# When the output projection follows the normalization, and which engine copies the convolution's image into PSUM

## The chip, the cores and the metric

The kernel runs on one core of one Trainium2 chip. The metric is the device time of one execution in microseconds; less is better. A profile of one execution is read beside it: busy times, waits and instructions of TensorE (PE), VectorE (DVE), ScalarE (ACT), GpSimd (POOL) and of the queue of SyncE (SP), which issues the transfers (DMA).

## The reference

Two layers on x of shape (4, 512, 64, 64), all in float32. Cut to what matters:

```python
# layer 0: attention over the 4096 pixels of an image, 128 channels inside
q, k, v = conv1x1(x, wq) + bq, conv1x1(x, wk) + bk, conv1x1(x, wv) + bv
attn = softmax(q^T k)                        # 4096 x 4096 for each of the 4 images
x = conv1x1(v attn^T, wo) + bo + x
# layer 1: involution, a 7x7 convolution whose weights are computed at each pixel
o = relu(conv1x1(x, W1) * s1 + b1)           # 128 channels in 8 groups of 16
w = conv1x1(relu(conv1x1(o, Wr) * sr + br), Ws) + bs     # 8 x 49 weights per pixel
o[c] = sum over 49 taps of w[group(c), tap] * shifted(o[c], tap)
x = conv1x1(o, W3) * s3 + b3 + x
```

## The kernel before

Each image (a batch) begins with its keys and values. Then its queries are worked through in 8 chunks of 512 pixels (8 image rows). For one chunk, 32 steps each make a score tile `pss`, its exponential `pt` on ScalarE, and add `v` times `pt` to `po` on TensorE; VectorE adds the exponentials into `pacc`. When the 32 steps are over, `finish_chunk` normalizes, projects and computes the tap weights; `involution` multiplies and adds the 49 taps; `close_chunk` projects and stores. These three are generators. They are not run at once: after each step of a later chunk, `chores` lets each of them make one turn, so that their instructions lie among those of the attention.

```python
    def takes(engine, us):
        free[engine] = max(free[engine], pe) + us
        return free[engine]
# ...
    def pace():
        nonlocal due, seen
        due, seen = min(due + TAPS_A_US * (pe - seen), 10), pe
        for _ in range(2):
            if due < 1 or not step(taps, 1):
                break
            due -= 1
# ...
    def chores():
        step(finishing, 1)
        step(closing, 1)
        pace()
```

`step` makes a turn of a generator; a turn that yields "wait" ends it without using up what is due. `pe` is the TensorE time issued so far by the kernel's own book, and `free` the time until which each of the others is booked. They decide only in which order instructions are issued.

The taps read the image `po1` from PSUM (8 rows and a border of 3 on each side). It is copied there from `o1` in SBUF: 11 rows at first, the last 3 when the next chunk's rows are known (`ready`). The weights of 7 taps come in one transfer `wb` of 1792 KB, read from the DRAM scratch `wsp`, into one of three buffers; two are loaded ahead.

```python
    def involution(b, c, o1):
        top = RW + PAD

        po1 = ps1.tile([P, RW + 2 * PAD, W + 2 * PAD], F32, tag="o1", name=f"po1_{b}_{c}")
        for _ in range(2):
            yield "wait"
        nc.scalar.copy(po1[:, :top], o1[:, :top])
        yield "wait"
        # ...
        for tap in range(NTAP):
            dy, dx = divmod(tap, K)
            if dx == 0:
                if dy == PAD + 1:
                    while (b, c) not in ready:
                        yield "wait"
                    yield "wait"
                    nc.scalar.copy(po1[:, top:], o1[:, top:])
                    yield "wait"
                wb, landed = loaded.pop(0)
                pump()
            while "tail" not in ready and (
                pe < landed or free["dve"] > pe + 3.0 or free["pool"] > pe + 6.0
            ):
                yield "wait"
            free["pool"] = max(free["pool"], takes("dve", DVE_OP))
            takes("pool", POOL_OP)
            prod = acc
            if tap:
                prod = prods.tile([P, RW, W], F32, tag="prod", name=f"prod_{b}_{c}_{tap}")
            nc.vector.tensor_tensor(
                prod, po1[:, dy : dy + RW, dx : dx + W],
                wb[:, dx, :].rearrange("p (r w) -> p r w", r=RW), ALU.mult,
            )
            if tap and "tail" in ready and tap % 2 and tap < NTAP - 2:

                first = accp is None
                if first:
                    accp = ps1.tile([P, CH], F32, tag="po", name=f"accp_{b}_{c}")
                mm(
                    accp, ident, prod.rearrange("p r w -> p (r w)"),
                    start=first, stop=tap == NTAP - 4,
                )
            elif tap:
                nc.gpsimd.tensor_tensor(acc, acc, prod, ALU.add)
            yield
```

The normalization takes the reciprocals of the sums, stores one row of them for a later check, and multiplies. The projection `pwo` follows after two turns:

```python
    def finish_chunk(b, c, o1s, po, sums):
        xt = xb[b, c]
        on = work2.tile([P, CH], F32, tag="on", name=f"on_{b}_{c}")
        nc.scalar.copy(on, po)
        for _ in range(3):
            yield
        pl = ps.tile([P, CH], F32, tag="mm", name=f"pl_{b}_{c}")
        mm(pl, ones, sums)
        rl = work1.tile([P, CH], F32, tag="rl", name=f"rl_{b}_{c}")
        for i in range(4):
            yield
            cols = slice(i * P, (i + 1) * P)
            takes("dve", 0.9)
            nc.vector.reciprocal(rl[:, cols], pl[:, cols])
        nc.sync.dma_start(rls[b * NCH + c : b * NCH + c + 1, :], rl[:1, :])
        takes("dve", DVE_OP)
        nc.vector.tensor_tensor(on, on, rl, ALU.mult)
        for _ in range(2):
            yield
        for t in range(CT):
            pw = ps.tile([P, CH], F32, tag="mm", name=f"pwo_{b}_{c}_{t}")
            mm(pw, w_slice(O_WO, t), on)
            takes("dve", DVE_OP)
            nc.vector.scalar_tensor_tensor(
                xt[:, t, :], pw, bo[:, t : t + 1], xt[:, t, :], ALU.add, ALU.add
            )
            yield
            if t % 2:
                yield
        p1 = ps.tile([P, RW, W], F32, tag="mm", name=f"p1_{b}_{c}")
        for t in range(CT):
            mm(
                p1.rearrange("p r w -> p (r w)"), w_slice(O_W1, t), xt[:, t, :],
                t == 0, t == CT - 1,
            )
            if t == 1:
                yield
        # ... relu, the image o1, the tap weights wc, their transfer to wsp,
        # and taps.append(involution(b, c, o1)) at its end
```

Once the last attention is over ("tail"), the taps go on with every other addition on TensorE instead of GpSimd.

Of the kernel before, what the change touches and what calls it, by code (L numbers as in the profile page):

```python
# [59 lines left out]
def fast_path(  # L60
# [18 lines left out]
    nc = tc.nc  # L79
# [41 lines left out]
# [3 lines that stand above are left out]
# [15 lines left out]
    def w_slice(off, t):  # L139
        return wt[:, off + t * P : off + (t + 1) * P]  # L140

    def v1(i):
        return vec[:, i : i + 1]

    def mm(o, lhsT, rhs, start=True, stop=True, shared=1):
        pe_us(rhs.free_size() * PE_COLUMN / shared)
        nc.tensor.matmul(o, lhsT=lhsT, rhs=rhs, start=start, stop=stop)  # L147
# [19 lines left out]
    def pump():  # L167
        while pending and len(loaded) < 2:
            wsp, written, i, name = pending.pop(0)
            wb = wbpool.tile([P, PIECE, CH], F32, tag="wb", name=name)  # L170
            nc.sync.dma_start(
                wb,
                wsp.rearrange("(g k) n -> g k n", g=G)[:, i * PIECE : (i + 1) * PIECE, :]
                .unsqueeze(0).broadcast_to([GC, G, PIECE, CH]),
            )
            free["dma"] = max(free["dma"], written)
            loaded.append((wb, takes("dma", PIECE_US) + LAND_US))
# [7 lines left out]
    def involution(b, c, o1):  # L185
        top = RW + PAD

        po1 = ps1.tile([P, RW + 2 * PAD, W + 2 * PAD], F32, tag="o1", name=f"po1_{b}_{c}")
        for _ in range(2):
            yield "wait"  # L190
        nc.scalar.copy(po1[:, :top], o1[:, :top])
        yield "wait"
        acc = work2.tile([P, RW, W], F32, tag="acc", name=f"acc_{b}_{c}")
        accp = None
        for tap in range(NTAP):
            dy, dx = divmod(tap, K)
            if dx == 0:
                if dy == PAD + 1:
                    while (b, c) not in ready:
                        yield "wait"  # L200
                    yield "wait"
                    nc.scalar.copy(po1[:, top:], o1[:, top:])
                    yield "wait"
                wb, landed = loaded.pop(0)
                pump()
            while "tail" not in ready and (
# [24 lines that stand above are left out]
        if accp is not None:  # L231
            nc.vector.tensor_tensor(
                acc, accp.rearrange("p (r w) -> p r w", r=RW), acc, ALU.add
            )
        closing.append(close_chunk(b, c, acc))
# [67 lines left out]
    def new_o1(b, c):  # L303
        o1 = o1pool.tile([P, RW + 2 * PAD, W + 2 * PAD], F32, tag="o1", name=f"o1_{b}_{c}")
        nc.gpsimd.memset(o1[:, :, :PAD], 0.0)
        nc.gpsimd.memset(o1[:, :, PAD + W :], 0.0)
        if c == 0:
            nc.gpsimd.memset(o1[:, :PAD, PAD : PAD + W], 0.0)
        if c == NCH - 1:
            nc.gpsimd.memset(o1[:, PAD + RW :, PAD : PAD + W], 0.0)  # L310
        return o1
# [16 lines that stand above are left out]
        nc.sync.dma_start(rls[b * NCH + c : b * NCH + c + 1, :], rl[:1, :])  # L328
        takes("dve", DVE_OP)
        nc.vector.tensor_tensor(on, on, rl, ALU.mult)  # L330
        for _ in range(2):
            yield
        for t in range(CT):
            pw = ps.tile([P, CH], F32, tag="mm", name=f"pwo_{b}_{c}_{t}")
# [3 lines that stand above are left out]
                xt[:, t, :], pw, bo[:, t : t + 1], xt[:, t, :], ALU.add, ALU.add  # L338
            )
            yield  # L340
            if t % 2:
                yield
        p1 = ps.tile([P, RW, W], F32, tag="mm", name=f"p1_{b}_{c}")
        for t in range(CT):
# [6 lines that stand above are left out]
        o1 = o1s[c]  # L351
        inner = o1[:, PAD : PAD + RW, PAD : PAD + W]
        nc.scalar.activation(inner, p1, AF.Relu, bias=v1(V_B1), scale=v1(V_S1))  # L353
        if c + 1 < NCH:
            o1s[c + 1] = new_o1(b, c + 1)
            nc.gpsimd.tensor_copy(  # L356
                o1s[c + 1][:, :PAD, PAD : PAD + W], o1[:, RW : RW + PAD, PAD : PAD + W]
            )
        if c > 0:
            nc.gpsimd.tensor_copy(  # L360
                o1s.pop(c - 1)[:, PAD + RW :, PAD : PAD + W], o1[:, PAD : 2 * PAD, PAD : PAD + W]
            )
        for t in range(CT):

            nc.scalar.activation(xt[:, t, :], xt[:, t, :], AF.Identity, bias=v1(V_B3 + t))  # L365
            if t % 2:
                yield
        pr = ps.tile([P, CH], F32, tag="mm", name=f"pr_{b}_{c}")
        mm(pr, wt[:, O_WR : O_WR + P], inner)
        red = work1.tile([P, CH], F32, tag="red", name=f"red_{b}_{c}")  # L370
        nc.scalar.activation(red, pr, AF.Relu, bias=v1(V_BR), scale=v1(V_SR))
        for _ in range(2):
            yield
        wc = work1.tile([P, 4, CH], F32, tag="wc", name=f"wc_{b}_{c}")
        for m0 in range(0, 4, 2):
            pcs = []
            for m in range(m0, m0 + 2):

                pc = ps.tile([P, CH], F32, tag="mm", name=f"pc_{b}_{c}_{m}")
                mm(  # L380
                    pc[:NWC, :], wt[CR * m : CR * (m + 1), O_WC : O_WC + NWC],
                    red[CR * m : CR * (m + 1), :], shared=2,
                )
                pcs.append(pc)
            for m, pc in zip(range(m0, m0 + 2), pcs):
                nc.scalar.activation(  # L386
                    wc[:NWC, m, :], pc[:NWC, :], AF.Identity,
                    bias=vec[:NWC, V_BC + m : V_BC + m + 1],
                )
            yield  # L390
        wsp = scratch.tile([4 * NWC, CH], F32, tag="wsp", name=f"wsp_{b}_{c}")
        written = takes("dma", WC_US) + LAND_US
        nc.sync.dma_start(wsp.rearrange("(m r) n -> r m n", m=4), wc[:NWC])
        pending.extend((wsp, written, i, f"wb_{b}_{c}_{i}") for i in range(NTAP // PIECE))
        pump()
        if c > 0:
            ready.add((b, c - 1))
        if c == NCH - 1:
            ready.add((b, c))
        taps.append(involution(b, c, o1))  # L400


# [458 lines left out]
```

## Time and profile before

| | |
|---|---|
| time, median of 3 | 2904.59 us (2897.92 to 2905.29) |
| span of the profiled execution | 2896.9 us |
| mean granted TensorE clock | 0.972 |
| one score or value product (2 passes) | 1.02 us, one each 0.86 us |
| ScalarE copy to `po1`, 11 rows (128x770) | 32 of 805 ns, 25.8 us |
| ScalarE copy to `po1`, 3 rows (128x210) | 32 of 338 ns, 10.8 us |
| one tap on VectorE, `prod` (128x512) | 1536 of 681 ns, 1001.0 us |
| one addition of a tap on GpSimd, `acc` | 1488 of 1270 ns, 1889.9 us |
| reciprocals `rl` on VectorE (128x128) | 128 of 929 ns, 115.6 us |

A line of a wait list says which engine and line waited for which other engine and line, then the us in total, the number of times and the longest. A line of a timeline has the start in us, the duration, engine, line, operation, tiles out<-in, shapes and how many it merges; in brackets stand the idle time just before it and who ended it. L330 is the multiplication `on`, L202 and L191 are the two copies to `po1`, L147 is every matmul. "PEld" is the load of TensorE's weights.

### The profile page before, as it was taken

How to read it: one execution, taken by the hardware profiler on the slowest of the kernel's cores; microseconds unless marked ns; L12 is line 12 of the kernel's file. 1: busy time of each engine (PE TensorE's matmuls, PEld its weight loads, DVE VectorE, ACT ScalarE, POOL GpSimd, SP SyncE). 2: the span in 40 equal slices, each digit the busy share in tenths (PEclk: the TensorE clock that was granted, in tenths of full speed). 3: DMA queues.
4: the chain of work that ended last, by engine and by line, in shares of the span. 5: the costliest groups of instructions: out<-in, count | busy, mean ns of one | idle time of the engine just before them, and what ended most of it. 6: DMA issues, size and time to landing. Idle time of an engine off the chain costs nothing.

```text
span 2896.9 us, 23193 instructions
## 1 busy us (share of the span) xinstructions
PE 2702.9 (93%) x6250; PEld 1150.1 (40%) x6250; DVE 1919.7 (66%) x3016; ACT 954.5 (33%) x1569; POOL 1916.3 (66%) x1623
## 2 busy tenths in 40 slices
PE   8999999999899999999989999999989999999975
PEld 4444443343344444443434444443334444444421
DVE  0447777876456777777464777777636577777864
ACT  2333333332233333333223333333233333333310
POOL 0028877777734877887780777778865288777744
PEclk9999999999999999999999999999999999999987
DMA  6048888889937988888991989998895588888896
GB/s 213 15 100 180 205 202 194 202 200 226 237 84 183 198 199 202 199 202 203 253 215 41 213 199 207 204 202 206 213 242 139 123 201 201 201 189 189 188 229 167
DMA packets 97532, 540.84 MB, mean 187 GB/s; under 512 B 6640, under 2 KB 6768, under 8 KB 68592
## 3 DMA queue, kind: packets, MB, share of 16 engines
q1 hardware_dynamic: 97104, 538.01, 79.5%
q8 instruction: 51, 0.84, 0.1%
q10 hardware_dynamic: 288, 1.27, 0.1%
q14 instruction: 89, 0.73, 0.1%
HBM read 479.94 MB, written 59.24 MB: 186 GB/s over the span
## 4 chain that ended last, share of the span: by engine, by line
PE 37%; DMA 33%; POOL 14%; DVE 10%; issue 5%; ACT 1%; SPq 0%; POOLq 0%; DVEq 0%; ACTq 0%
DMA wb<-wsp 31%; POOL acc L229 13%; PE pss L147 11%; PE po L147 11%; PE py L147 4%; DVE pacc L439 4%; PE p L147 4%; DVE prod L215 3%; PE pwo L147 3%; DVE rl L327 2%; DMA wsp<-wc 2%; PE pv L147 1%; PE pk L147 1%; PE pq L147 1%; DMA out_dram<-xb 0%
## 5 line engine op out<-in xcount | busy, mean ns | idle before, releaser
L229 POOL TENSOR_TENSOR acc<-acc,prod 128x512 f32<-128x512 f32 x1488 | 1889.9, 1270 | 462.5 <-DVE prod L215 317.7
L215 DVE TENSOR_TENSOR prod<-po,wb 128x512 f32<-128x512 f32 x1536 | 1001.0, 681 | 281.5 <-DMA wb<-wsp 200.9
L147 PE MATMUL pss<-q,k 128*128 128x512 f32 x2048 | 1070.5, 605 | 34.5 <-ACT pt L414 34.5
L147 PE MATMUL po<-pt,v 128*128 128x512 f32 x2048 | 1063.0, 602 | 0.0
L414 ACT ACTIVATE pt<-pss 128x512 f32<-128x512 f32 x1024 | 610.5, 597 | 1255.1 <-PE pss L147 1128.4
L439 DVE TENSOR_TENSOR pacc<-pacc,pt 128x512 f32<-128x512 f32 x960 | 662.1, 690 | 289.9 <-ACT pt L414 287.1
L147 PEld LDWEIGHTS pss<-q,k 128*128 128x128 f32 x2048 | 387.2, 192 | 555.2 <-issue 485.0
L147 PEld LDWEIGHTS po<-pt,v 128*128 128x128 f32 x2048 | 393.0, 193 | 506.0 <-issue 487.9
L356 POOL COPY o<-o 128x192 f32<-128x192 f32 x28 | 9.7, 348 | 463.2 <-ACT o L353 317.4
L147 PE MATMUL pwo<-on,wt 128*128 128x512 f32 x256 | 143.1, 643 | 80.6 <-DVE on L330 78.3
L246 DVE SCALAR_TENSOR_TENSOR xb<-py,vec,xb 128x512 f32<-128x512 f32 x128 | 95.4, 745 | 100.5 <-PE py L147 99.7
L147 PE MATMUL py<-acc,wt 128*128 128x512 f32 x256 | 136.5, 620 | 22.1 <-DVE xb L337 12.1
L215 DVE TENSOR_TENSOR acc<-po,wb 128x512 f32<-128x512 f32 x32 | 22.1, 692 | 187.9 <-DMA wb<-wsp 187.8
L147 PE MATMUL pk<-xa,wt 128*128 128x512 f32 x256 | 122.7, 618 | 3.5 <-DMA xa<-x_dram 3.5
L365 ACT ACTIVATE xb<-xb,vec 128x512 f32<-128x512 f32 x128 | 91.9, 718 | 91.9 <-PE p L147 87.4
L147 PE MATMUL p<-xb,wt 128*128 128x512 f32 x256 | 120.1, 592 | 0.0
L147 PE MATMUL pv<-xa,wt 128*128 128x512 f32 x256 | 118.3, 600 | 0.0
L327 DVE RECIPROCAL rl<-pl 128x128 f32<-128x128 f32 x128 | 115.6, 929 | 1.6 <-PE pl L147 1.6
L147 PE MATMUL pq<-xb,wt 128*128 128x512 f32 x256 | 115.7, 592 | 0.0
L147 PEld LDWEIGHTS pwo<-on,wt 128*128 128x128 f32 x256 | 50.5, 207 | 160.2 <-DVE on L330 101.2
L386 ACT ACTIVATE wc<-pc,vec 98x512 f32<-98x512 f32 x128 | 81.2, 684 | 80.1 <-PE pc L147 80.1
L337 DVE SCALAR_TENSOR_TENSOR xb<-pwo,bo,xb 128x512 f32<-128x512 f32 x128 | 94.5, 740 | 14.8 <-PE pwo L147 14.5
(50 smaller groups left out, 822.2 us busy)
## 6 DMA issues: line engine op xcount, KB each, us to landing
wb<-wsp SPq DMA_DIRECT2D x224, 1792.0 KB
xa<-x_dram SPq DMA_DIRECT2D x32, 1024.0 KB
xb<-x_dram SPq DMA_DIRECT2D x32, 1024.0 KB
out_dram<-xb SPq DMA_DIRECT2D x32, 1024.0 KB
wsp<-wc SPq DMA_DIRECT2D x32, 784.0 KB
wt<-wts_dram ACTq DMA_DIRECT2D x1, 1137.0 KB
wt<-wts_dram SPq DMA_DIRECT2D x1, 512.0 KB
rls<-rl SPq DMA_DIRECT2D x32, 2.0 KB
```

Source lines behind the costliest of these rows:

```text
L147: nc.tensor.matmul(o, lhsT=lhsT, rhs=rhs, start=start, stop=stop)
L215: nc.vector.tensor_tensor(prod, po1[:, dy : dy + RW, dx : dx + W], wb[:, dx, :].rearrange("p (r w) -> p r w", r=RW), ALU.mult,)
L229: nc.gpsimd.tensor_tensor(acc, acc, prod, ALU.add)
L246: nc.vector.scalar_tensor_tensor(xt[:, t, :], py, v1(V_S3 + t), xt[:, t, :], ALU.mult, ALU.add)
L327: nc.vector.reciprocal(rl[:, cols], pl[:, cols])
L337: nc.vector.scalar_tensor_tensor(xt[:, t, :], pw, bo[:, t : t + 1], xt[:, t, :], ALU.add, ALU.add)
L356: nc.gpsimd.tensor_copy(o1s[c + 1][:, :PAD, PAD : PAD + W], o1[:, RW : RW + PAD, PAD : PAD + W])
L365: nc.scalar.activation(xt[:, t, :], xt[:, t, :], AF.Identity, bias=v1(V_B3 + t))
L386: nc.scalar.activation(wc[:NWC, m, :], pc[:NWC, :], AF.Identity, bias=vec[:NWC, V_BC + m : V_BC + m + 1],)
L414: nc.scalar.activation(pt, pss, AF.Exp)
L439: nc.vector.tensor_tensor(paccs[c], paccs[c], pt, ALU.add)
```

## The change

It has two parts. In `finish_chunk`, five turns instead of two pass between the normalization and the first `pwo`, and the second turn after a `pwo` now follows the tiles 0, 2 and 3 instead of 1 and 3. In `involution`, VectorE copies the image to `po1` instead of ScalarE; the copies are booked for VectorE, and the turns in which the taps waited around a copy are gone. The first part gives VectorE more time to come to the end of the normalization before TensorE needs it. The second keeps ScalarE's queue free of an instruction that waits for VectorE.

```diff
--- before.py
+++ after.py
@@ -186,10 +186,8 @@
         top = RW + PAD
 
         po1 = ps1.tile([P, RW + 2 * PAD, W + 2 * PAD], F32, tag="o1", name=f"po1_{b}_{c}")
-        for _ in range(2):
-            yield "wait"
-        nc.scalar.copy(po1[:, :top], o1[:, :top])
-        yield "wait"
+        takes("dve", 0.8)
+        nc.vector.tensor_copy(po1[:, :top], o1[:, :top])
         acc = work2.tile([P, RW, W], F32, tag="acc", name=f"acc_{b}_{c}")
         accp = None
         for tap in range(NTAP):
@@ -198,9 +196,8 @@
                 if dy == PAD + 1:
                     while (b, c) not in ready:
                         yield "wait"
-                    yield "wait"
-                    nc.scalar.copy(po1[:, top:], o1[:, top:])
-                    yield "wait"
+                    takes("dve", 0.3)
+                    nc.vector.tensor_copy(po1[:, top:], o1[:, top:])
                 wb, landed = loaded.pop(0)
                 pump()
             while "tail" not in ready and (
@@ -328,7 +325,7 @@
         nc.sync.dma_start(rls[b * NCH + c : b * NCH + c + 1, :], rl[:1, :])
         takes("dve", DVE_OP)
         nc.vector.tensor_tensor(on, on, rl, ALU.mult)
-        for _ in range(2):
+        for _ in range(5):
             yield
         for t in range(CT):
             pw = ps.tile([P, CH], F32, tag="mm", name=f"pwo_{b}_{c}_{t}")
@@ -338,7 +335,7 @@
                 xt[:, t, :], pw, bo[:, t : t + 1], xt[:, t, :], ALU.add, ALU.add
             )
             yield
-            if t % 2:
+            if t != 1:
                 yield
         p1 = ps.tile([P, RW, W], F32, tag="mm", name=f"p1_{b}_{c}")
         for t in range(CT):
```

## The prediction

> **What bounds the kernel now.** I read the page from the top: busy time first, then the waits of the engine that is busiest, then the timeline around its longest waits.
>
> ```profile
> PE 2702.9 (93%) x6250; PEld 1150.1 (40%) x6250; DVE 1919.7 (66%) x3016; ACT 954.5 (33%) x1569; POOL 1916.3 (66%) x1623
> ```
>
> TensorE (PE) is busy 93% of the span; its 194 us of idle are what a reordering can win or lose. The other engines have a third of their time free, so work moved between them costs time only where TensorE then waits. The chain that ended last puts 31% on the loads `wb<-wsp`, but it runs back from the end through the tail, so I use it for the tail alone. From 200 to 2700 us (all of the attention but the first chunk and the last) TensorE waits for:
>
> ```profile
> PE pwo L147 <- DVE on L330: 75.6, 26, 3.6
> PE pss L147 <- ACT pt L414: 33.9, 12, 6.2
> PE py L147 <- DVE xb L337: 12.1, 10, 1.4
> ```
>
> The columns are us in total, times, longest. Idle in that stretch is 2500 - 2367.8 = 132 us, and the first line is more than half of it. It recurs once a chunk, 2.9 us a time: the output projection `pwo` waits for the multiplication `on`, which is the end of the normalization on VectorE. The timelines of TensorE and of VectorE in one chunk show it:
>
> ```profile
> 1072.02 1.02 PE L147 MATMUL po<-pt,v 128*128 128x512 f32 x2
> 1076.54 1.13 PE L147 MATMUL pwo<-on,wt 128*128 128x512 f32 x2 [3.50 <-DVE on L330]
> 1077.50 1.63 PE L147 MATMUL pss<-q,k 128*128 128x512 f32 x2
> ```
> ```profile
> 1075.81 0.68 DVE L330 TENSOR_TENSOR on<-on,rl 128x512 f32<-128x512 f32 x1
> ```
>
> TensorE's matmuls stand one behind another at 0.86 us until `pwo`; nothing behind it can start, although scores are ready. VectorE is busy all of 1070 to 1080 us (10.00 of 10 us) with four reciprocals, additions and taps, so `on` simply comes late. Second, at the start of a batch ScalarE is what holds up the scores. Its copy of the image's lower rows waits, and the exponentials stand behind it:
>
> ```profile
> 787.75 0.34 ACT L202 COPY po<-o 128x210 f32<-128x210 f32 x1 [7.36 <-DVE prod L215]
> ```
> ```profile
> 788.67 2.07 PE L147 MATMUL pss<-q,k 128*128 128x512 f32 x2 [4.75 <-ACT pt L414]
> ```
>
> This happens in the three later batches (4.75, 2.85 and 4.65 us of TensorE). In each of them a longer stop comes some 18 us earlier (5.60, 6.22, 6.09 us), where VectorE waits for tap weights and `pacc` stands behind the taps; the change does not address that one.
>
> **What the Trainium skill says.** "TensorE: Matmul & The Clock Gate", section "What's actually happening", says that an idle window of about 3.4 us halves the TensorE clock until activity releases it. The trace agrees: the pair after the 4.75 us stop takes 2.07 us instead of 1.02, and after stops of 2 to 3.6 us at `pwo` some pairs take 2.07 and some 1.13. So a stop costs more than its length. The same page, section "Architectural detail", says that ScalarE and VectorE queues are strictly first in, first out; the 787.75 us line shows it. "VectorE: DVE Perf Modes", section on the TRN2 errata, gives (N+151)/0.96 ns for an fp32 addition, and "Why PSUM operands drop a tier" says that an fp32 operand in PSUM leaves no faster mode. At 512 elements that is 691 ns; the trace has 681 to 692 for the taps and 684 for the copy `pacc<-pt` into PSUM. I use the formula for the new copies, as an estimate.
>
> **The change, part by part.**
>
> *Three more steps before `pwo`.* A step of the attention is two matmul pairs, 2 x 0.86 = 1.7 us of TensorE at least. Now `pwo` comes two steps after `on` is issued and waits up to 3.6 us; three more steps are 5.1 us at least. That covers the longest wait seen, so nearly all of the 78.3 us of the whole run (27 waits) should go: **-74 us**, with 4 left for chunks in which VectorE falls further behind. In the windows 850:1350, 1550:2050 and 2250:2750 the granted clock is 0.99, 0.99 and 0.98; about 1.3% of 2500 us is 33 us, part of it while TensorE idles or at the batch starts. I count **-13 us** for matmuls that no longer run slow after a `pwo` stop.
>
> *The copies on VectorE.* ScalarE loses 25.8 + 10.8 = 36.6 us of work and its 115.2 + 60.7 us of waits. Most of that was free: in mid-batch the upper copy waits 2.85 us just before `q`, beside a 3.6 us matmul group. What counts is the three stops above, 12.3 us plus slow restarts of 1 to 3 us. VectorE needs no wait for its own earlier taps. **-11 us**. VectorE gains 32 x (0.96 + 0.38) = 43 us (estimate: 770 and 210 elements by the formula). Its mid-batch share goes from some 72% to 77%, but it is full during the normalization, and a late `pacc` holds the five `pt` buffers and then TensorE. I put **+7 us** on the path.
>
> *No gap in the taps.* Five idle turns per chunk (three around the upper copy, two around the lower) go. I expect no gain here: taps are behind TensorE in mid-batch. The order of the built programs even shows the taps later than before. When the last attention chunk of a batch ends, before has issued taps up to number 41 of chunk 5, after only to 29. Two things do that: each chunk's tap weights start later (below), and VectorE's larger booked load makes taps yield.
>
> *A later end of each chunk.* The projection now has seven turns instead of six, so the end of `finish_chunk` comes 3 + 1 = 4 steps later; at 78.4 us per chunk (the copies at 1043.82 and 1122.24) and 32 steps that is 9.8 us. In mid-batch this is only a shift. At the end it is not: from 2742 us, where chunk 6's tap weights are written to DRAM, to the end 155 us pass, and 14 loads of 1792 KB (25.7 MB) at the 197 GB/s of that window need 130 us. This stretch hangs on the start of its loads, so it starts 9.8 us later against the attention's end: **+10 us**. The same lateness puts four more taps between the end of a batch and the next batch's first score (53 instead of 49 in the program orders), where DMA is at 98% already; the stops of about 6 us there may grow: **+6 us** over three batches.
>
> Sum: -74 - 13 - 11 + 7 + 10 + 6 = -75; 2904.6 - 75 = 2830. I take **2827**, because removing a stop also spares the scores behind it a slow clock that I counted low.
>
> **Rivals.** *DMA becomes the bound.* A chunk moves 7 x 1.835 MB of tap weights, 0.8 to DRAM and 2.1 of x and output, 15.7 MB. At the 211 to 216 GB/s of its full windows this takes 74 us; a chunk would then last 78.4 - 3.5 = 75. For it: the margin is small, and VectorE already waits 200.9 + 187.8 us for these loads. Against it: DMA moves x faster (up to 274 GB/s), and its share is 0.83 over 500 us. If it holds, half the gain is lost: 2865. *VectorE takes the place of the wait.* Between steps 8 and 16 of a chunk the new order puts 14 taps where there were 10, right where `on` and the four `xb` updates are due. If `pwo` still waits 1 to 2 us, or the scores wait for `pt`, the gain is 35 us: 2870. *The tail and batch starts take it all back:* that would need 75 us, seven times what I find; the time would be 2900. *All of it is won:* no residual wait and none of the +7 and +6: 2800.
>
> **Range and chances.** The main term rests on a repeated, simple wait and a margin of 5.1 against 3.6 us; the signs of the small terms are clear, their sizes are not. The rivals together weigh about a quarter. Range 2796 to 2862. Faster by 2% means below 2846.5: 0.76. Within 2%: 0.22. Slower: 0.02.
>
> **What would show it.** Right: TensorE's wait `pwo` for `on` falls from 78.3 us to below 10; the granted clock in mid-batch reaches 1.00; the distance from chunk to chunk falls from about 78 to about 75 us; ScalarE has no copy of the image and the second stop of a batch start is gone; VectorE's busy time rises by about 40 us; from the end of the last score to the end of the span some 10 us more pass than now (136 from 2761 us). Wrong: `pwo` still waits, now for a VectorE that is full; TensorE waits for `pt` in mid-batch; VectorE's waits for `wb` grow by far and DMA stands at 1.0 without a break; the tail grows by two or more loads.

## The result and the profile after

The changed kernel takes 2833.93 us (median; 2823.35 to 2836.07), 0.9749 of the time before, with a 95% interval of 0.9716 to 0.9782. The profiled execution has a span of 2831.6 us against 2896.9. The line of busy times in the page of the changed kernel:

```profile
PE 2686.0 (95%) x6262; PEld 1150.2 (41%) x6262; DVE 1945.6 (69%) x3080; ACT 926.3 (33%) x1505; POOL 1908.9 (67%) x1617
```

TensorE's idle time fell from 194 to 146 us, and its busy time by 17 us although it has slightly more to do (12 more records, six more additions of taps in the tail). What it waits for between 200 and 2640 us (us in total, times, longest):

```profile
PE pc L147 <- DVE xb L243: 18.5, 4, 7.7
PE pq L147 <- ACT wc L383: 14.7, 19, 0.8
PE py L147 <- DVE xb L243: 14.4, 3, 8.9
PE py L147 <- DVE xb L334: 11.1, 7, 3.4
PE py L147 <- ACT wc L383: 10.8, 14, 0.8
PE pss L147 <- ACT pt L411: 8.8, 5, 2.2
PE pwo L147 <- DVE xb L334: 5.0, 3, 1.9
```

The wait of `pwo` for `on`, 75.6 us before, is no longer in the list, and the scores' wait for `pt` fell from 33.9 to 8.8. New at the top is a small number of long stops. The timelines of VectorE and of TensorE around one `pwo` in mid-batch:

```profile
1054.00 0.68 DVE L327 TENSOR_TENSOR on<-on,rl 128x512 f32<-128x512 f32 x1
```
```profile
1057.45 1.02 PE L147 MATMUL po<-pt,v 128*128 128x512 f32 x2
1058.31 1.02 PE L147 MATMUL pwo<-on,wt 128*128 128x512 f32 x2
1059.17 1.02 PE L147 MATMUL pss<-q,k 128*128 128x512 f32 x2
```

`on` ends at 1054.7 us and `pwo` starts at 1058.31, 0.86 us after the matmul ahead of it: no gap, and no slow matmul behind it. VectorE's groups show the two new copies:

```profile
L190 DVE COPY po<-o 128x770 f32<-128x770 f32 x32 | 30.6, 956 | 8.7 <-ACT o L350 8.5
L200 DVE COPY po<-o 128x210 f32<-128x210 f32 x32 | 12.1, 379 | 69.1 <-POOL o L357 68.9
```

956 and 379 ns: the estimate was 960 and 380.

To see where the time went I divide every span by the starts of ScalarE's copy `on<-po`, of which there is one at the end of each chunk's attention. "Mid-batch" is the sum of the 28 distances inside the batches, "batch starts" that of the three from the last copy of a batch to the first of the next (they hold the keys and values and the next batch's first chunk), "tail" the time from the last copy to the end. The first 135 to 136 us, up to the first copy, are left out.

| us, one profile each | mid-batch | batch starts | tail | span |
|---|---|---|---|---|
| before | 2130.0 | 494.7 | 136.2 | 2896.9 |
| changed | 2038.3 | 512.5 | 145.7 | 2831.6 |
| difference | -91.7 | +17.8 | +9.5 | -65.3 |

A chunk in mid-batch takes 72.8 us instead of 76.1 on average. The 91.7 us come from two sources, and TensorE has the same number of matmul records there (4727 and 4728): its idle time in mid-batch fell from 86.7 to 28.2 us, by 58.5, and its busy time from 2043.2 to 2010.2 us, by 33.0. Four middle chunks of the second batch show it, before and after (start and end, length, then busy us and records of PE, PEld, DVE, ACT and POOL, the granted clock, the DMA share and GB/s):

```profile
979.90:1293.30 313.40, 298.40 (x689) 126.80 (x688) 237.16 (x376) 112.39 (x184) 248.78 (x212) 0.98 0.88 202
```
```profile
963.90:1263.80 299.90, 293.71 (x689) 125.66 (x688) 242.11 (x387) 108.63 (x177) 248.51 (x211) 1.00 0.91 209
```

In these chunks the changed kernel's TensorE is busy 98% of the time at a granted clock of 1.00. The batch starts, which I had expected to gain, lost. The new long stops lie there; this is one of them, on TensorE and on VectorE:

```profile
710.60 2.02 PE L147 MATMUL pc<-red,wt 32*98 32x512 f32 x2 [7.68 <-DVE xb L243]
```
```profile
708.60 1.29 DVE L212 TENSOR_TENSOR prod<-po,wb 128x512 f32<-128x512 f32 x2 [8.41 <-DMA wb<-wsp]
709.81 0.74 DVE L243 SCALAR_TENSOR_TENSOR xb<-py,vec,xb 128x512 f32<-128x512 f32 x1
```

VectorE stood for 8.41 us at a tap whose weights had not landed. The update `xb` behind it would have emptied a PSUM tile, and `pc` was waiting for that tile. It is the same kind of stop as before the change (a tap without weights holds up what stands behind it in VectorE's queue), with another victim. Of the eight waits for `xb` that are longer than 2 us, the four longest (8.9, 7.7, 6.0 and 3.9 us) have such a tap ahead of them; the other four, of 2.2 to 3.4 us, do not.

### The profile page after: what moved, and what is told of

Its sections match the earlier page's. It is cut to its first block, busy times and chain, and to the rows that moved or that the text cites. A ratio compares the mean times of both kernels' runs of the same rounds, so it can differ in the third digit from the quotient of the medians.

```text
span 2831.6 us, 23290 instructions
## 1 busy us (share of the span) xinstructions
PE 2686.0 (95%) x6262; PEld 1150.2 (41%) x6262; DVE 1945.6 (69%) x3080; ACT 926.3 (33%) x1505; POOL 1908.9 (67%) x1617
## 4 chain that ended last, share of the span: by engine, by line
PE 70%; DMA 18%; DVE 6%; issue 2%; POOL 2%; ACT 1%; SPq 0%; DVEq 0%; POOLq 0%; ACTq 0%
PE pss L147 25%; PE po L147 25%; DMA wb<-wsp 17%; PE py L147 3%; PE p L147 3%; DVE prod L212 3%; PE pwo L147 3%; PE pq L147 3%; PE pc L147 2%; DVE pacc L436 2%; PE pv L147 2%; POOL acc L226 2%; PE pk L147 1%; ACT wc L383 1%; PE pr L147 1%
## 5 line engine op out<-in xcount | busy, mean ns | idle before, releaser
L147 PE MATMUL pss<-q,k 128*128 128x512 f32 x2048 | 1050.9, 595 | 8.8 <-ACT pt L411 8.8
L147 PE MATMUL po<-pt,v 128*128 128x512 f32 x2048 | 1048.8, 594 | 0.0
L147 PE MATMUL py<-acc,wt 128*128 128x512 f32 x256 | 141.1, 638 | 43.5 <-DVE xb L243 14.4
L147 PE MATMUL pwo<-on,wt 128*128 128x512 f32 x256 | 131.2, 595 | 5.0 <-DVE xb L334 5.0
L147 PE MATMUL pv<-xa,wt 128*128 128x512 f32 x256 | 125.7, 631 | 0.0
L147 PE MATMUL accp<-prod,ident 128*128 128x512 f32 x108 | 69.7, 787 | 32.3 <-DVE prod L212 32.0
L147 PE MATMUL pc<-red,wt 32*98 32x512 f32 x256 | 80.9, 652 | 19.3 <-DVE xb L243 18.5
```

## The experiments

Each kernel is given as its difference from the changed kernel. All medians are in the table; the ratios are to the kernel before, measured beside each set. Each stage is read from one profile, and repeats of a whole kernel differ by 1 to 22 us (by 13 us for the changed kernel), so a few us between two stages are no finding.

| kernel | us | ratio (95%) | mid-batch | batch starts | tail |
|---|---|---|---|---|---|
| changed | 2833.9 | 0.9749 (0.9716-0.9782) | 2038.3 | 512.5 | 145.7 |
| steps only | 2863.6 | 0.9862 (0.9844-0.9880) | 2071.3 | 492.6 | 162.6 |
| copies only | 2899.8 | 0.9980 (0.9964-0.9997) | 2114.1 | 509.5 | 139.2 |
| ScalarE, no gap | 2864.1 | 0.9863 (0.9844-0.9882) | 2046.8 | 537.2 | 143.1 |
| VectorE, with gaps | 2845.4 | 0.9812 (0.9784-0.9839) | 2052.7 | 484.9 | 162.5 |
| one more step | 2857.4 | 0.9850 (0.9830-0.9871) | 2060.6 | 517.3 | 137.5 |
| last chunks early | 2840.9 | 0.9787 (0.9771-0.9804) | 2045.8 | 508.2 | 143.3 |
| copies twice | 2837.3 | 0.9771 (0.9749-0.9792) | 2062.1 | 486.9 | 148.6 |
| load booked 8.7 us | 2837.3 | 0.9772 (0.9755-0.9790) | 2060.1 | 493.9 | 147.6 |
| gaps but last batch | 2825.2 | 0.9718 (0.9691-0.9745) | 2056.4 | 489.1 | 146.0 |
| the same, longer book | 2836.7 | 0.9762 (0.9735-0.9790) | 2067.3 | 487.4 | 144.5 |
| longer book only | 2834.6 | 0.9760 (0.9728-0.9792) | 2042.5 | 510.5 | 144.1 |
| all three | 2826.2 | 0.9738 (0.9704-0.9772) | 2062.7 | 489.3 | 134.6 |

### The two parts apart

Theory: the gain is the wait of `pwo` for `on`; engine and gaps are small. Rivals: the gaps matter, or the engine does.

**Steps only.** `involution` is that of the kernel before.

```diff
-        takes("dve", 0.8)
-        nc.vector.tensor_copy(po1[:, :top], o1[:, :top])
+        for _ in range(2):
+            yield "wait"
+        nc.scalar.copy(po1[:, :top], o1[:, :top])
+        yield "wait"
         # and the lower rows with one turn ahead and one behind, as before
```

> Only the turns of the normalization and projection are changed; ScalarE copies with its gaps, as before. Theory A (the gain is the wait of pwo for on, and nothing else counts): that wait near 0, time within 15 us of the changed kernel's 2834, so 2825 to 2850. Rival B (the gaps matter once each chunk ends later: five idle turns of the taps no longer fit into a chunk): wait of pwo near 0 too, but the taps fall behind; in the order of the program the last attention ends with 15 taps of chunk 5 issued against 29 in the changed kernel, two loads of tap weights more in the tail, so the tail is 15 to 20 us longer than the changed kernel's 146 and the time 2855 to 2880.

2864 us, 30 us over the changed kernel and in rival B's range: the theory, as I put it, fails. The wait for `on` is gone, and the tail is 17 us longer, as rival B said. But mid-batch is longer too, by 33 us, which neither had.

**Copies only.** The turns of `finish_chunk` are those of the kernel before.

```diff
-        for _ in range(5):
+        for _ in range(2):
             yield
-            if t != 1:
+            if t % 2:
                 yield
```

> Only the copies are changed (VectorE, no gap); the turns of the normalization and projection are as before. Theory A: the wait of pwo for on stays at 78 us or grows a little with VectorE's 43 us of new work; the second stop at the batch starts (12 us) goes; time 2890 to 2905. Rival (the copies bring a good part of the gain, as ScalarE no longer holds exponentials back in mid-batch): below 2875.

2900 us, hardly faster than before. TensorE's waits in this kernel:

```profile
PE pwo L147 <- DVE on L327: 64.5, 27, 3.6
PE pss L147 <- ACT pt L411: 25.0, 6, 7.6
```

With the two turns the wait for `on` stays, 27 times. So the steps make the gain, and the copies alone do not; but together they bring 30 us more than the steps alone. The next two runs say which half of the second part that is.

**ScalarE copies, no gap.**

```diff
-        takes("dve", 0.8)
-        nc.vector.tensor_copy(po1[:, :top], o1[:, :top])
+        nc.scalar.copy(po1[:, :top], o1[:, :top])
-                    takes("dve", 0.3)
-                    nc.vector.tensor_copy(po1[:, top:], o1[:, top:])
+                    nc.scalar.copy(po1[:, top:], o1[:, top:])
```

> The changed kernel with both copies on ScalarE again, still without a gap in the taps. The taps stand further on at the end of the last attention than in the changed kernel (37 of chunk 5 against 29). Theory A (the engine counts little, ScalarE's stops at the batch starts come back): those stops 10 to 20 us in all, 2835 to 2855. Rival B (the engine is what counts: exponentials stand behind a copy that waits for the taps, in every chunk): TensorE's wait for pt above 40 us, time over 2865. Rival C (VectorE's 43 us of copies cost more than ScalarE's stops): below 2828.

2864 us: without gaps the engine is worth 30 us, more than the 20 of my first guess and close to the rival B's limit. (The booking of the copies for VectorE goes with the engine, and with it the order of the taps; the two were not tried apart.) It is only in small part the rival's mechanism: 24.7 us lie in the batch starts and 8.5 in mid-batch. TensorE's waits:

```profile
PE pss L147 <- ACT pt L409: 33.0, 26, 3.8
...
PE pk L147 <- DMA xa<-x_dram: 21.3, 7, 4.5
```

and ScalarE's timeline in the first batch start:

```profile
726.21 0.80 ACT L189 COPY po<-o 128x770 f32<-128x770 f32 x1 [7.76 <-DVE prod L210]
...
777.53 0.34 ACT L198 COPY po<-o 128x210 f32<-128x210 f32 x1 [6.30 <-DVE prod L210]
```

ScalarE stands 7.76 and 6.30 us at its copies. This is the stop I had seen before the change; it comes back. Of the 33.0 us that the scores wait for `pt`, 19.0 lie in the three batch starts; the rest are some 20 short waits, spread over the chunks as rival B said. The keys' wait for x (`pk`, 21.3 us against 3.5 in the changed kernel) comes on top; why the loads of x are later here was not followed up.

**VectorE copies, with gaps.**

```diff
         takes("dve", 0.8)
+        for _ in range(2):
+            yield "wait"
         nc.vector.tensor_copy(po1[:, :top], o1[:, :top])
+        yield "wait"
         # and one turn ahead of and one behind the lower copy
```

> The changed kernel with VectorE's copies, but with the five idle turns of the taps put back. Theory A (the gaps cost nothing): 2825 to 2845. Rival B (they cost because the chunk now ends later): the last attention ends with 13 taps of chunk 5 issued against 29, the tail is 15 to 20 us longer and the batch starts carry some 20 taps more: 2855 to 2885.

2845 us, some 11 us over the changed kernel by the medians, at the upper edge of theory A's range and below rival B's. The stages show two effects of opposite sign. With gaps the tail is 16.8 us longer, and so is mid-batch (14.4); the batch starts are 27.6 us shorter. The ScalarE pair (steps only against no gap) has the same signs: 19.5 and 24.5 longer, 44.6 shorter, and no difference in sum. Read the other way, the same four kernels give the engine 18 us with gaps (2863.6 against 2845.4) and 30 without, and with gaps 18.6 of them lie in mid-batch and 7.7 at the batch starts: engine and gaps do not simply add. The order of the programs explains the direction: with gaps 13 taps of chunk 5 are issued when the last attention ends, without them 29. Taps that are behind are left over for the tail; that they also ask for fewer loads while the keys and values are made would explain the batch starts, but is not shown by itself.

### How many steps

**One more step** than before: three turns, and the old ones between the `pwo`.

```diff
-        for _ in range(5):
+        for _ in range(3):
-            if t != 1:
+            if t % 2:
```

> The changed kernel with three turns instead of five before the first pwo, and the old turns between the pwo: one more than before, so the chunk ends one step later and not four. The wait of pwo for on was 2.9 us a time; a step is 1.7 us of TensorE at least. Theory A (each step takes its own length off the wait): some 1.2 us a time or 30 to 35 us in all are left, the tail is about 2.5 us longer than before's 136, time 2850 to 2872. Rival (one step is enough, since other matmuls lie in it too): the wait is below 10 us, the chunk ends earlier than in the changed kernel, and the time is below 2834.

The time, 2857, is in the theory's range, but for another reason. TensorE's waits:

```profile
PE py L147 <- DVE xb L334: 43.7, 16, 9.2
...
PE pwo L147 <- DVE on L327: 1.1, 2, 0.5
```

A single step already removes the wait for `on`, so theory A's account is wrong and the rival's wait is right, though not its time. The stop moves to the next thing VectorE owes: `xb`, which empties the PSUM tile that `py` needs (`pwo` and `py` share two buffers with other tiles). Of the 43.7 us, 17.2 lie in mid-batch (2.5 in the changed kernel) and 26.5 at the batch starts (8.5). The larger change needs its other steps for that. Whether it is the turns ahead of the first `pwo` or the changed ones between them was not separated.

### The tail

**Last chunks early:** the last two chunks of the last batch keep two turns and the old ones between the `pwo`.

```diff
-        for _ in range(5):
+        for _ in range(2 if b == B - 1 and c >= NCH - 2 else 5):
             yield
-            if t != 1:
+            if t != 1 and not (b == B - 1 and c >= NCH - 2) or t % 2 and b == B - 1 and c >= NCH - 2:
                 yield
```

> The changed kernel, but the last two chunks of the last batch keep the old turns (two before pwo). Theory A (the tail hangs on the start of the loads for chunk 6, which four steps delay by some 10 us): tail 136 to 140 us instead of 146, one or two stops of 3 us come back, time 4 to 9 us below the changed kernel's. Rival (the tail is bound by the taps that the last batch is behind, 29 against 41 of chunk 5): the tail stays within 3 us of 146 and the time within 3 us of 2834.

The tail is 143.3, within 3 us of 146: theory A fails here, and the time does not fall (2841, 7 us above the changed kernel, which the rival did not have either; its profile's span is 2832.9). The windows of the first 50 us of the tail, here and in the changed kernel (columns as above):

```profile
2689.60:2739.60 50.00, 40.92 (x87) 15.46 (x85) 37.11 (x59) 7.45 (x11) 27.54 (x22) 0.93 0.83 207
```
```profile
2685.90:2735.90 50.00, 41.77 (x86) 16.54 (x85) 37.46 (x59) 7.55 (x11) 26.66 (x22) 0.85 1.01 242
```

Chunk 6's first load is issued 19.5 us ahead of the end of the attention (2670.09 against 2689.6 us) instead of 8.3. But the third is issued 9.8 us behind that end in both kernels (at 2699.42 and at 2695.73 us), and DMA's share of the window is 0.83 instead of 1.01. In the program two loads are ahead of the taps, and the next is issued when the taps take up a buffer; so taps that are behind hold the loads back.

**Longer book only** lets taps be issued further ahead in the last batch:

```diff
-                pe < landed or free["dve"] > pe + 3.0 or free["pool"] > pe + 6.0
+                pe < landed or free["dve"] > pe + (4.5 if b == B - 1 else 3.0) or free["pool"] > pe + 6.0
```

> The changed kernel with 4.5 instead of 3.0 us of booking ahead in the last batch and nothing else. Everything up to the last batch is issued as in the changed kernel; 37 taps of chunk 5 instead of 29 at the end of its attention. Theory A (taps that are behind make the tail): tail 139 to 142 instead of 146, time 2825 to 2832. Rival (the start of chunk 6's loads makes it): tail and time as in the changed kernel.

Tail 144.1, time 2835: eight taps fewer behind, and nearly no gain, as the rival said. Neither cause alone shortens the tail by more than 2 us.

### The batch starts

**Copies twice.** Both lines of each copy stand twice (booked twice too).

> The changed kernel with both copies made (and booked) twice: 32 x (0.95 + 0.37) = 42 us more of VectorE. It measures what such work costs. Theory A (VectorE has slack, little of it is on the path): 5 to 12 us, so 2837 to 2848. Rival (VectorE is full where it matters): 25 to 42 us, so 2858 to 2876. If it costs nothing or gains, the taps' later place (27 against 33 of chunk 6 issued when a batch's scores begin) eases the batch starts.

2837 us, not to be told from the changed kernel: another 42 us of VectorE, booked, cost next to nothing. The batch starts are 26 us shorter and mid-batch is 24 us longer, which is what the gaps do too; it may be the booking, but work and booking were not tried apart.

**Load booked 8.7 us.**

```diff
-PIECE_US, X_US, WC_US, LAND_US = 7.4, 3.8, 3.6, 3.5
+PIECE_US, X_US, WC_US, LAND_US = 8.7, 3.8, 3.6, 3.5
```

> The changed kernel with one number of its own book changed: a load of tap weights is booked with 8.7 us, which is what back-to-back loads take in the trace, instead of 7.4. In mid-batch the order of the taps hardly changes; at a batch start 20 taps of chunk 6 are issued before the first score instead of 33. Theory A (the batch starts are long because VectorE takes up taps whose weights have not landed, and what stands behind them waits): from the last on of a batch to the first of the next 161 to 166 us instead of 171 on average, time 10 to 28 us below the changed kernel's 2834. Rival (DMA is the bound there whatever the order): same time within 5 us, the stops only move to the loads of x.

2837 us. The batch starts did fall by 19 us, but mid-batch grew by 22. And the stops of `pc` became longer, not fewer:

```profile
PE pc L147 <- DVE xb L243: 37.1, 5, 12.5
```

The gain of theory A was given back; where, stands under "Open" below.

**Gaps but last batch.** The kernel with gaps, for `b < B - 1` alone (the copies are booked ahead of the gaps here, not behind them).

> The changed kernel with the idle turns of the taps put back in the first three batches and left out in the last. Theory A (the gaps trade the tail against the batch starts: taps that are behind press fewer loads into the keys and values, but lengthen the tail): batch starts as in the kernel with all gaps (485 us for the three), mid-batch 2040 to 2052, tail as in the changed kernel (146), so 2808 to 2824. Rival (the stages do not add up this way; what is left out at the batch starts comes back in mid-batch): 2830 to 2845.

2825 us, the lowest median of all, but its interval overlaps the changed kernel's: clearly faster than before, not clearly faster than the change. It lies between the ranges of theory and rival: batch starts and tail are about as the theory said (489.1 and 146.0), and mid-batch gave back 18 us (2056.4), as the rival said.

**The same, with the longer book** in the last batch.

> As the run before, and in the last batch alone the taps may be issued while VectorE is booked up to 4.5 us ahead instead of 3.0. The last attention then ends with 37 taps of chunk 5 issued instead of 29. Theory A (the tail grows by the taps that are behind, some 0.8 us for each): tail 139 to 142 us, time 5 us below the run before. Rival (the tail hangs on when chunk 6's weights are ready): tail stays at 145 to 147.

2837, tail 144.5: a miss. The last batch's own chunks became 8 us longer (523.2 against 514.9).

**All three:** gaps in three batches, the longer book, and the last chunks early.

> The kernel with gaps in three batches and the longer booking in the last, and the last two chunks with the old two turns before pwo. With the taps further on, chunk 6's loads can now use their earlier start. Theory A (an earlier end of chunk 6 only helps once the taps are not behind): tail 133 to 138 us, time 3 to 8 us below the kernel without it. Rival (the earlier end does not matter, its stops at pwo cost 3 us each): same time within 3 us or more.

The tail is 134.6 us, as theory A said: 10 us below the kernel without the last of the three. The time is 2826, 11 us below it, more than theory A had. The longer book and the early chunks were combined only in this kernel, with the gaps in the first three batches. SyncE's queue shows the loads of the tail, in the changed kernel and in this one (`wb` are the tap weights; x4 is four loads merged):

```profile
2672.45 0.32 SPq L390 DMA_DIRECT2D wsp<-wc  x1
2677.62 0.51 SPq L171 DMA_DIRECT2D wb<-wsp  x1
...
2678.82 0.51 SPq L171 DMA_DIRECT2D wb<-wsp  x1
...
2695.73 9.39 SPq L171 DMA_DIRECT2D wb<-wsp  x2
```
```profile
2669.49 0.34 SPq L398 DMA_DIRECT2D wsp<-wc  x1
2673.87 19.48 SPq L171 DMA_DIRECT2D wb<-wsp  x4
```

The attention ends at 2686 and 2687 us in the two. By 2694 us the changed kernel has issued two loads of chunk 6, the other one four; at 25.7 MB for 14 loads and some 200 GB/s a load is 9 us, so the lead is some 18 us, of which 11 are left as gain over the changed kernel's tail.

## Why the prediction was right, and where it was not

Predicted were 2827 us, measured 2834, inside the range and below the 2% line. The main step, a wait that more turns remove, is right. That the sum fits as closely as it does is luck: errors of opposite sign met in it. The steps one by one:

- **The wait of `pwo` for `on` (-74 us): right, but not all of it is gain.** It went from 78.3 us to nothing that TensorE's list shows, and with the old turns it stays (64.5 us in "copies only"). The margin was larger than I reckoned: one step is enough for `on`. What I did not see is that the next wait, for `xb`, was behind it; with one step it takes 43.7 us. And in mid-batch, where the wait was 70.7 us, TensorE's idle time fell by only 58.5: short waits of `pq` and `py` for ScalarE's `wc`, at most 0.8 us each, came up from 2.3 to 24.7 us.
- **The clock (-13 us): right mechanism, too small.** With the same matmuls TensorE's busy time in mid-batch fell by 33.0 us, and the granted clock in the four chunks shown above rose from 0.98 to 1.00. I had reckoned 33 us and then counted less than half of it. Over the whole run the busy time fell by 17 us, since it grew by 6.7 us at the batch starts and by 10.4 in the tail.
- **ScalarE's stops (-11 us): right mechanism, wrong size.** With the steps in place the engine is worth 30 us without gaps, 24.7 of them at the batch starts, and 18 with gaps. The longer stops some 18 us earlier, which I had said the change does not address, ended too: the longest wait of a score for `pt` is now 2.2 us.
- **VectorE's new work (+7 us): at most that.** The copies measured 42.7 us of the 43 estimated; twice as many of them, with their booking, cost 3 us, within the measurement. VectorE's busy time in the page rose by only 26 us: overlapping instructions count once there, and the sum of all durations rose by 41.
- **"No gap: I expect no gain": wrong for VectorE.** The gaps cost mid-batch and tail 14 and 17 us and save 28 at the batch starts. I had looked only at the sum of the taps against TensorE, not at when they ask for their weights. In sum leaving them out is worth some 11 us by the medians (4 by the two profiles), and nothing while ScalarE copies.
- **The batch starts (-11 + 6): wrong sign.** They grew by 17.8 us. The stops that ended with the change (scores behind `pt`) were replaced by `pc` and `py` behind `xb`, and the longest of these stand behind a tap whose weights have not landed. The failed step is the +6 for the later end of each chunk: "steps only" has that later end, and its batch starts are 492.6 us, 2 less than before; "copies only" has the old turns, and they are 509.5. Leaving out the gaps makes them longer (by 44.6 us with ScalarE's copies, 27.6 with VectorE's); that was not in my sum.
- **The tail (+10 us): right number, half of the reason.** 9.5 us. I had put it down to the four steps by which chunk 6 ends later. Taking those back alone gave 2 us, bringing the taps forward alone 2 us, both together 11.

By stage I had some -80 for mid-batch (if the first two steps and VectorE's work are put there whole), -5 for the batch starts and +10 for the tail. Mid-batch gained 12 us more than that and the batch starts lost 23 us more, so 10 of the 75 us were missing in the profiles (7 us against the 2827, by the medians). I had also taken one chunk of 78.4 us for all; the average of mid-batch was 76.1.

Of the rivals none held for the kernel as a whole. The chunks of 75 us in the four shown above are hardly longer than the 74 us that I had reckoned for their loads, but TensorE waits only 2% of that time and the DMA share is 0.91, not 1. "VectorE takes the place" held for the kernel with one more step.

Open: why three kernels that shorten the batch starts by 19 to 26 us (copies twice, load booked 8.7, gaps but last batch) each lose 18 to 24 in mid-batch. For two of them the traces show where. In the changed kernel each batch start holds eight `py` matmuls, which close two chunks, and the second distance of the batch behind it holds at most half a one. With the load booked 8.7 us, four of the eight have moved on, and four lie in that second distance. The second distances of the three later batches add up to 233.5 us instead of 212.6: that is 20.9 of the 21.8 us lost. With gaps but the last batch they are 229.2 us, 16.6 of the 18.1 lost, and the two kernels with gaps throughout show the same (227.5 and 233.0). So a part of these gains is work that has crossed the line at which I divide: twelve `py` of 0.86 us are 10 of the 19 us in the case of the booked load. The rest comes with waits of 2.4 to 2.8 us of `py` for `xb`. In "copies twice" only 3.4 of the 23.7 us lie there, and its loss stays open.

## What to carry to other kernels

When an in-order engine waits for another engine's result, give the producer more turns, and then look at the next result that the same producer owes: the wait may only move on. Keep instructions that wait for a lagging engine out of the queue of a third one, above all of one that feeds the busiest. And divide the span into stages before judging a reordering, and see whether the same work still lies in each: here leaving out the gaps helped two stages and hurt the third by nearly as much, in part because work crossed a line, and the tail yielded only when both of its causes were removed together.

## What the runs showed of the hardware

A second set of copies, 42 us of VectorE's time, moved the total by 3 us, within the measurement, when it was booked as well: VectorE's busy share went from 69 to 70%. A VectorE copy of 770 fp32 elements from SBUF to PSUM took 956 ns where ScalarE took 805, and 379 ns against 338 for 210 elements; the kernel was the faster with VectorE's copies, by 18 us with gaps and by 30 without. The 689 matmul records of four chunks kept TensorE busy 298.4 us with the stops at `pwo` and 293.7 us without them.
